# Attention in a fused layer: value products in every second step, from three tiles of turned exponentials

## The chip, the cores and the metric

The kernel runs on one core of one Trainium2 chip. The metric is the device time of one execution in microseconds (us). A core has five engines that run side by side, each with its own queue: TensorE (PE) multiplies matrices, VectorE (DVE) and ScalarE (ACT) work on elements, GpSimd (POOL) here issues the gathers by index, and SyncE (SP) issues most other transfers. PEld is PE's weight load, shown apart from the matmuls.

## The reference, cut to what matters

Two sequences of 4096 rows of 512 numbers go through a layer norm. Its result `xn` feeds an attention and a mixture of 16 experts, and the output is the sum of the input, the attention and the experts. All numbers are float32.

```
q, k, v = projections of xn, 64 wide, q and k rotated by position
scores = where(causal, q @ k.T / 8, -1e30)
attn = softmax(scores, axis=-1)
o = attn @ v
out_attention = o @ W_comp2lat.T @ W_to_kv + (o @ W_comp2lat.T) @ W_out_res.T + b_out_res
out_experts = shared expert + two of 16 experts per row, weighted
x = x + out_attention + out_experts
```

## The kernel before, in words

The work comes in four stages on one core. The first (to about 760 us) does norm, router, shared expert and projections. The second is a first attention pass over `p` = 0 to 6. The third is the experts (`gate_up`, `down`). The fourth is a second attention pass over `p` = 7 to 15, into which the last sums are woven. Both passes are one function, `attention` (line 773), called at lines 964 and 1137.

One `p` stands for two blocks of 128 queries in both sequences. Keys come in blocks of 128 too, and causality leaves `n = 2p + 2` of them. They are worked off two at a time, so a `p` has `M = p + 1` steps: 28 steps in the first pass, 108 in the second. A step does, in this order:

- `exps`: exponentials on ACT that this step needs and that are still waiting (line 756 works one piece of up to 1024 columns);
- `turn` (line 781): 16 small transposes on PE (line 790) of exponentials `E` into a PSUM tile `et` in two halves, and one copy per half to the SBUF tile `eT` (lines 796, 798, 799) on ACT, every fifth on DVE (every second for `p` = 15), as `copies` says. The halves take three PSUM banks in turn (`bank_of_three`);
- the sums that are due (`combine`, line 1104), in the second pass alone;
- a share of the scores of the next `p`: a chunk is 4 matmuls (line 740) and two reductions on DVE (lines 745, 748); the last two steps of a `p` have none, nor has `p` = 15;
- up to two exponentials of the next `p`;
- `products` (line 802) of the step before: 8 matmuls (line 810) that add `vv` times `eT` to the PSUM tile `oT`. After the last step of a `p`, DVE copies `oT` to `qT` (line 812). `oT` has one buffer.

The list `late` holds the one step whose products are still to come. PE, DVE and ACT keep the order in which the code names instructions (`manual_schedule`); SP's and POOL's order is made by a planner when the program is built, from its estimates and the free buffers.

`combine(p, i)` (due at the steps of line 1126: two for every seven) multiplies `qT` by `WO` (`po`, line 1112), and on DVE adds the rows of the experts and of `acc_d` (lines 1116, 1118); SP writes them out (line 1119). `load_parts` (line 1083) loads `acc_d` into tiles `fac` (line 1093, 12 buffers, four per `p`) and gathers two expert rows per token from `y_d` on POOL (line 1098): for `i` = 0 both are added onto `fac`, for `i` = 1 both go to a tile `fyy` of four. A group of four gathers therefore serves one `combine`: two for the first expert, two for the second, which add to what the first have brought. A half below is one `combine(p, i)`, part `p` with `i` = 0 or 1.

Of the kernel before, what the change touches and what calls it, by code (L numbers as in the profile page):

```python
# [8 lines left out]
F32 = mybir.dt.float32  # L9
# [10 lines left out]
P = 128  # L20
NB, T, D = 2, 4096, 512
# [31 lines left out]
def tile_mla_then_moe(  # L53
# [44 lines left out]
    def psO(name, second=False):  # L98
        return ps.tile([P, 512], F32, tag="T" if second else "O", name=name, bufs=1)
# [37 lines left out]
    at = ctx.enter_context(tc.tile_pool(name="at", bufs=2))  # L137
# [542 lines left out]
    def exps(n, upto=None):  # L680

        while waiting and (n > 0 or (upto is not None and min(waiting)[0] <= upto)):
            e = min(waiting)
            waiting.remove(e)
            e[2]()
            n -= 1
# [22 lines left out]
    def copies(p):  # L709

        turns[1] += 1
        return V.tensor_copy if turns[1] % (5 if p + 1 < NPR else 2) == 0 else S.copy
# [58 lines left out]
    H = P // 2  # L771

    def attention(E_tile, first, last, rows, extras, banks, copies, E_read=lambda t: None):

        late = []

        def turn(p, js, eT, n):

            pt = banks(f"et{p}_{js[0]}")
            for u, j in enumerate(js):
                for b in range(NB):
                    for i in range(1 if j == n - 1 else 0, 2):
                        o = u * 256 + (b * 2 + i) * H
                        for h in range(2):
                            e = slice(h * H, (h + 1) * H)
                            tr(pt[h][:, o:o + H],  # L790
                               rows[i][j // 8][e, b, (j % 8) * P:(j % 8 + 1) * P], ident[e, e])
            for h in range(2):
                copy = copies(p)
                dst = eT.rearrange("p u h b i q -> p (u h) (b i q)")
                if js[1] < n - 1:
                    copy(dst[:, h:h + 3:2, :], pt[h].rearrange("p (u c) -> p u c", u=2))  # L796
                else:
                    copy(dst[:, h, :], pt[h][:, 0:256])
                    copy(eT[:, 1, h, :, 1, :],
                         pt[h][:, 256:].rearrange("p (b i q) -> p b i q", b=NB, i=2)[:, :, 1, :])  # L800

        def products(p, oT, js, eT, n):
            for u, j in enumerate(js):
                for b in range(NB):
                    o, e = oT[b * DC:(b + 1) * DC, 0:256], eT[:, u, :, b]
                    if j == n - 1:
                        o, e = o.rearrange("d (h i q) -> d h i q", h=2, i=2)[:, :, 1], e[:, :, 1]
                    else:
                        e = e.rearrange("p h i q -> p h (i q)")
                    mm(out=o, lhsT=vv[j // 4][:, b, j % 4, :], rhs=e, start=(j == 0), stop=(j == n - 1))  # L810
            if js[-1] == n - 1:
                V.tensor_copy(
                    qT[p // 2][:, (p % 2) * 256:(p % 2 + 1) * 256].rearrange("d (i h q) -> d i h q", i=2, h=2),
                    oT[:, 0:256].rearrange("d (h i q) -> d i h q", h=2, i=2))

        for p in range(first, last):
            nxt, steps = score_steps(E_tile, p + 1, bank_pair) if p + 1 < last else (None, [])
            oT = psO(f"oT{p}")
            more = extras(p)
            n, M = 2 * p + 2, p + 1  # L820
            early = max(1, M - 2)
            pieces = sum(NB * -(-(n + 1 + i) // 8) for i in (0, 1)) if p + 1 < last else 0
            turn_of = 0.0
            for m in range(M):
                js = [2 * m, 2 * m + 1]

                exps(0, (p, min(js[1] + 2, n - 1) // 8))
                eT = at.tile([P, 2, 2, NB, 2, H], F32, tag="eT", name=f"eT{p}_{m}", bufs=2)
                turn(p, js, eT, n)
                for j in js:  # L830
                    if j % 8 == 7 or j == n - 1:
                        for i in range(2):
                            E_read(rows[i][j // 8])
                for f in more[len(more) * m // M:len(more) * (m + 1) // M]:
                    if f:
                        f()
                if m < early:
                    for f in steps[len(steps) * m // early:len(steps) * (m + 1) // early]:
                        f()
                turn_of = min(turn_of + pieces / M, 2.0)  # L840
                exps(int(turn_of), (p + 1, 0) if m == M - 1 else None)
                turn_of -= int(turn_of)
                if late:
                    late.pop()()
                late.append(lambda p=p, oT=oT, js=js, eT=eT, n=n: products(p, oT, js, eT, n))
            rows = nxt
        late.pop()()

    ring_k = ctx.enter_context(tc.tile_pool(name="rk", bufs=4))
    on_way = tc.tile_pool(name="wx", bufs=1)
    wx = on_way.__enter__()
# [106 lines left out]
    def fill(p):  # L961
        return filling.get(p, [])

    attention(E_first, 0, NPA, rows, fill, bank_of_three, copies)
    ring_a.__exit__(None, None, None)

# [101 lines left out]
    fin = ctx.enter_context(tc.tile_pool(name="fin", bufs=2))  # L1068
# [9 lines left out]
    def E_read(t):  # L1078
        live[:] = [e for e in live if e[1] is not t]
# [3 lines left out]
    def load_parts(p):  # L1083


        if p >= NPR:
            return
        tiles = {}
        for i in range(2):
            for b in range(NB):  # L1090
                j = b * (NT // NB) + 2 * p + i
                t = fin.tile([P, D], F32, tag="ac", name=f"fac{j}", bufs=12)
                nc.sync.dma_start(out=t, in_=acc_d[j * P:(j + 1) * P, :])
                y = t if i == 0 else fin.tile([P, D], F32, tag="yy", name=f"fyy{j}", bufs=4)
                tiles[i, b] = j, t, y
        for k in range(TOPK):
            for j, t, y in tiles.values():
                G.indirect_dma_start(  # L1098
                    out=y, out_offset=None, in_=y_d,
                    in_offset=bass.IndirectOffsetOnAxis(ap=pos[k][:, j:j + 1], axis=0),  # L1100
                    compute_op=ALU.bypass if y is not t and k == 0 else ALU.add)
        parts[p] = tiles

    def combine(p, i):

        if i == 0:
            load_parts(p + 2)
        qb = 2 * p + i
        po = psA(f"po{qb}")
        for b in range(NB):  # L1110
            e = slice(b * DC, (b + 1) * DC)
            mm(out=po[:, b, :], lhsT=qT[p // 2][e, (qb % 4) * P:(qb % 4 + 1) * P], rhs=WO[e, :],
               start=True, stop=True)
        for b in range(NB):
            j, a, y = parts[p][i, b]
            V.scalar_tensor_tensor(a, po[:, b, :], rl[:, b, qb:qb + 1], a, ALU.mult, ALU.add)
            if y is not a:
                V.tensor_tensor(a, a, y, ALU.add)  # L1118
            nc.sync.dma_start(out=out[j * P:(j + 1) * P, :], in_=a)
# [15 lines left out]
    for p in range(2):  # L1135
        load_parts(p)
    attention(E_rest, NPA, NPR, rows, sums_of, bank_of_three, copies, E_read)
    for i in range(2):
        combine(NPR - 1, i)
# [41 lines left out]
```

## Time and profile before

| | |
|---|---|
| median of 11 runs | 1978.75 us (1974.4 to 1984.36) |
| the profiled execution | 1978.63 us, span 1976.4 |
| busy in the span: PE, PEld, DVE, ACT, POOL | 96%, 71%, 55%, 32%, 29% |
| granted TensorE clock, mean | 0.992 |
| value matmuls, line 810 | 1088, of them 1024 on 256 columns: 393 ns each |
| transposes, line 790 | 2112, 231 ns each |
| copies of `eT` on ACT, line 796 | 186, 586 ns each |
| gathers of `fac`, of `fyy`, line 1098 | 64 each, 1570 and 1265 ns each |

The profile is one execution. A matmul's duration includes its way through the array, and matmuls overlap, so their cost is read from start to start. In a timeline a row is: start, duration of the merged instructions, engine, line, operation, output<-input, shapes, count, and in brackets how long the engine had stood idle and what is taken to have released it. In a list of waits a row is: engine and what it wanted, what it waited for, the total, the number of times and the longest.

### The profile page before, as it was taken

To read this page: it belongs to the slowest core of one execution; us is meant where nothing else is said; L and a number is where in the kernel's file an instruction comes from. 1 tells how busy PE (TensorE), PEld (TensorE's weight loads), DVE (VectorE), ACT (ScalarE), POOL (GpSimd) and SP (SyncE) were. 2 spreads that over 40 slices of the span, in tenths; PEclk is the share of its full clock that TensorE was granted. 3 is DMA by queue.
4 is the path that set the end of the run, shared out by engine and by line. 5 is a ranking of instruction groups with operands and counts; after the bars stand their busy time and mean duration, and the time that the engine had idled before them with its cause. 6 is when DMAs were issued, how large, how long until landed. Compare 5 with 4: busy or idle time off the path is not lost. (4 is left out here: it accounts for less than half of the span.)

```text
span 1976.4 us, 31902 instructions
## 1 busy us (share of the span) xinstructions
PE 1889.2 (96%) x12242; PEld 1404.7 (71%) x12242; DVE 1077.9 (55%) x2910; ACT 638.8 (32%) x1069; POOL 571.3 (29%) x499
## 2 busy tenths in 40 slices
PE   7999999999999987899999999999999999999996
PEld 6888888888888865467777777777777674444453
DVE  8878777778778776632222222222223325787774
ACT  2322232333222223531111111111111455666663
POOL 2333333323233341111111111111111105454554
PEclk9999999999999989999999999999999999999998
DMA  6222222322122213147888877878887767888887
GB/s 233 65 76 65 75 86 76 97 82 79 65 75 65 75 43 124 34 136 249 272 289 272 276 264 269 297 254 284 279 274 239 242 223 200 202 201 196 202 207 189
DMA packets 219435, 342.42 MB, mean 173 GB/s; under 512 B 19204, under 2 KB 109952, under 8 KB 219280
## 3 DMA queue, kind: packets, MB, share of 16 engines
q1 hardware_dynamic: 167600, 234.09, 36.7%
q0 software_dynamic: 31696, 69.99, 14.1%
q10 hardware_dynamic: 19984, 36.25, 4.8%
q8 instruction: 99, 1.62, 0.4%
q14 instruction: 56, 0.46, 0.1%
HBM read 250.22 MB, written 90.05 MB: 172 GB/s over the span
## 5 line engine op out<-in xcount | busy, mean ns | idle before, releaser
L1009 PE MATMUL pg<-xt,wgu 128*128 128x256 f32 (+1 forms) x2816 | 496.1, 335 | 0.0
L1009 PEld LDWEIGHTS pg<-xt,wgu 128*128 128x128 f32 x2816 | 434.8, 191 | 43.0 <-issue 0.5
L931 POOL DMA_INDIRECT xg<-xn_d,table x137 | 130.5, 952 | 684.3 <-DVE sw L991 553.4
L1015 DVE TENSOR_TENSOR eh<-esg,pg 128x512 f32<-128x512 f32 (+1 forms) x69 | 47.2, 684 | 394.8 <-ACT esg L1014 394.8
L1023 PE MATMUL py<-wdn,eh 128*128 128x512 f32 x548 | 247.1, 594 | 0.0
L986 DVE COPY xt<-pxt 128x512 f32<-128x512 f32 x138 | 88.3, 682 | 176.7 <-PE pxt L983 176.6
L1023 PEld LDWEIGHTS py<-wdn,eh 128*128 128x128 f32 x548 | 102.2, 190 | 106.6 <-issue 98.5
L756 ACT ACTIVATE E<-E,nb 128x1024 f32<-128x1024 f32 (+7 forms) x160 | 160.3, 1004 | 42.5 <-DVE nb L751 42.4
L1027 ACT ACTIVATE y<-py,sw 128x512 f32<-128x512 f32 x137 | 94.1, 687 | 231.1 <-PE py L1023 203.0
L748 DVE TENSOR_SCALAR_CACHE_REDUCE E<-s 128x512 f32<-128x512 f32 x224 | 143.6, 686 | 42.9 <-PE s L740 33.6
L1014 ACT ACTIVATE esg<-pg 128x512 f32<-128x512 f32 (+1 forms) x69 | 41.0, 594 | 380.6 <-PE pg L1009 332.9
L740 PE MATMUL s<-kT,qT 64*128 64x512 f32 (+3 forms) x576 | 142.7, 593 | 11.3 <-DVE E L748 7.3
L392 POOL DMA_INDIRECT order_d<-tok,at_u x128 | 129.1, 1009 | 64.6 <-issue 35.5
L810 PE MATMUL oT<-eT,vv 128*64 128x256 f32 x1088 | 144.0, 386 | 3.8 <-DVE eT L796 2.5
L790 PEld LDWEIGHTS et<-ident,E 64*128 64x128 f32 x2112 | 80.8, 139 | 78.7 <-issue 49.2
L796 ACT COPY eT<-et 128x512 f32<-128x512 f32 x186 | 102.0, 586 | 102.0 <-PE et L790 67.1
L810 PEld LDWEIGHTS oT<-eT,vv 128*64 128x64 f32 x1088 | 66.6, 136 | 93.7 <-issue 31.9
L790 PE MATMUL et<-ident,E 64*128 64x64 f32 x2112 | 102.6, 231 | 24.5 <-ACT eT L796 14.3
L1098 POOL DMA_INDIRECT fac<-y_d,pos_all x64 | 100.5, 1570 | 78.9 <-DMA fac<-y_d,pos_all 63.2
L353 POOL TENSOR_TENSOR x<-x,b_bc 128x2048 f32<-128x2048 f32 x16 | 76.1, 4756 | 147.1 <-DVE xn L350 134.3
L1098 POOL DMA_INDIRECT fyy<-y_d,pos_all x64 | 81.0, 1265 | 115.6 <-ACT eT L796 54.4
L460 ACT ACTIVATE gs<-gs 128x512 f32<-128x512 f32 x64 | 40.3, 630 | 182.4 <-DVE gs L479 69.3
(245 smaller groups left out, 2868.0 us busy)
## 6 DMA issues: line engine op xcount, KB each, us to landing
wgu<-in_L_ffn_gate_w_dram SPq DMA_DIRECT2D x88, 512.0 KB, 6.0
wgu<-in_L_ffn_up_w_dram SPq DMA_DIRECT2D x88, 512.0 KB, 8.8
wdn<-in_L_ffn_down_w_dram SPq DMA_DIRECT2D x88, 512.0 KB, 4.1
y_d<-y ACTq DMA_DIRECT2D x137, 256.0 KB, 6.0
xn_d<-xn SPq DMA_DIRECT2D x16, 1028.0 KB, 4.8
x<-in_L_attn_x_dram SPq DMA_DIRECT2D x16, 1024.0 KB, 6.7
acc_d<-x SPq DMA_DIRECT2D x16, 1024.0 KB, 5.3
fac<-acc_d SPq DMA_DIRECT2D x64, 256.0 KB, 5.1
```

Of the source, the lines that this page charges most:

```text
L392: G.indirect_dma_start(out=order_d[n % 4], out_offset=bass.IndirectOffsetOnAxis(ap=at_u[:, i, k:k + 1], axis=0), in_=tok[:, g * 4 + i, k:k ...
L740: mm(out=sc[b][:, 0:w], lhsT=q[e, :], rhs=kT[c][e, 0:w], start=True, stop=True)
L748: V.tensor_scalar(dst, sc[b][:, 0:w], SCALE, None, ALU.mult, ALU.max, accum_out=m)
L756: S.activation(E, E, AF.Exp, bias=nb[:, b:b + 1], accum_out=sm[:, b, c:c + 1])
L790: tr(pt[h][:, o:o + H], rows[i][j // 8][e, b, (j % 8) * P:(j % 8 + 1) * P], ident[e, e])
L796: copy(dst[:, h:h + 3:2, :], pt[h].rearrange("p (u c) -> p u c", u=2))
L810: mm(out=o, lhsT=vv[j // 4][:, b, j % 4, :], rhs=e, start=(j == 0), stop=(j == n - 1))
L931: G.indirect_dma_start(out=x_n, out_offset=None, in_=xn_d, in_offset=bass.IndirectOffsetOnAxis(ap=table[:, n:n + 1], axis=0))
L1009: mm(out=pg[:, g, f, at_s], lhsT=weights[u][0][:, c, g * FE + f * P:g * FE + (f + 1) * P], rhs=x_u[:, c, :], start=(c == 0), stop=(c == 3))
L1023: mm(out=py[:, v, :], lhsT=hT[:, c, v * P:(v + 1) * P], rhs=weights[u][1][:, c, :], start=(c == 0), stop=(c == 1))
L1027: S.activation(y, py[:, v, :], AF.Copy, scale=slot_w.pop(n))
L1098: G.indirect_dma_start(out=y, out_offset=None, in_=y_d, in_offset=bass.IndirectOffsetOnAxis(ap=pos[k][:, j:j + 1], axis=0), compute_op=ALU ...
```

## The change

`products` is no longer called in each step for the step before. The steps are counted over a whole call of `attention`; after each even one the products of all held steps but the newest are issued, two steps in one batch (one the first time). What is left at the end of the pass is issued there. So up to three `eT` tiles are alive, and they come from a pool of their own with three buffers, opened ahead of the `E` tiles, in place of two in `at`. A buffer is 4 KB per partition. `fac` goes from 12 buffers to 10, at 2 KB each.

```diff
+        count = [0]
...
-                eT = at.tile([P, 2, 2, NB, 2, H], F32, tag="eT", name=f"eT{p}_{m}", bufs=2)
+                eT = turned_E.tile([P, 2, 2, NB, 2, H], F32, tag="eT", name=f"eT{p}_{m}")
...
-                if late:
-                    late.pop()()
                 late.append(lambda p=p, oT=oT, js=js, eT=eT, n=n: products(p, oT, js, eT, n))
+                count[0] += 1
+                if count[0] % 2 == 0:
+                    for f in late[:-1]:
+                        f()
+                    del late[:-1]
...
-        late.pop()()
+        for f in late:
+            f()
...
+    turned_E = ctx.enter_context(tc.tile_pool(name="te", bufs=3))
...
-                t = fin.tile([P, D], F32, tag="ac", name=f"fac{j}", bufs=12)
+                t = fin.tile([P, D], F32, tag="ac", name=f"fac{j}", bufs=10)
```

In the built program SP and POOL follow. A load of `fac` stands behind the write-out of the half five before it, where it stood behind the half six before. On POOL the groups of `fac` and `fyy` alternate as before, but a `fac` group stands one `fyy` group later; the last four groups are `fac`, `fyy`, `fac`, `fyy` in whole, where before the third and second from last were interleaved.

## The prediction

> **What bounds the kernel now.** The profiled execution took 1978.63 us: a span of 1976.4 and 2.2 around it. The median of the runs shown is 1978.75 (1974.4 to 1984.36), so it stands at the median. On the page PE is busy 96%, which covers four stages. The change touches the first attention pass (764.9 to 859.8 us: p = 0 to 6, 28 steps) and the second (1641.9 on: p = 7 to 15, 108 steps). The expert stage between them starts when the first pass leaves PE, so what the first pass gains or loses moves all that follows.
>
> First view: PE's timeline in the second pass.
>
> ```profile
> 1802.46 0.71 PE L790 MATMUL et<-ident,E 64*128 64x64 f32 x16
> 1803.00 1.08 PE L740 MATMUL s<-kT,qT 64*128 64x512 f32 x4
> 1804.01 1.08 PE L810 MATMUL oT<-eT,vv 128*64 128x256 f32 x8
> 1805.03 0.71 PE L790 MATMUL et<-ident,E 64*128 64x64 f32 x16
> ```
>
> From start to start: 0.54 us of transposes, 1.01 of scores, 1.02 of values, without a pause. It looks as if PE set the pace. Second view: POOL's timeline at the end.
>
> ```profile
> 1933.18 1.00 POOL L1098 DMA_INDIRECT fyy<-y_d,pos_all  x1 [0.31 <-issue]
> 1934.48 0.96 POOL L1098 DMA_INDIRECT fyy<-y_d,pos_all  x1 [0.30 <-DVE fac L1116]
> 1939.11 1.57 POOL L1098 DMA_INDIRECT fyy<-y_d,pos_all  x1 [3.67 <-DMA fyy<-y_d,pos_all]
> 1940.98 1.56 POOL L1098 DMA_INDIRECT fyy<-y_d,pos_all  x1 [0.30 <-issue]
> 1942.84 1.54 POOL L1098 DMA_INDIRECT fac<-y_d,pos_all  x1 [0.30 <-issue]
> ```
>
> A group is four gathers: two first ones, a wait until they have landed, two that add. Between groups POOL pauses 0.30 us, whatever releaser is named. Third view: who POOL waited for from 1646 us on.
>
> ```profile
> POOL fac L1098 <- DMA fac<-y_d,pos_all: 63.2, 21, 5.4
> POOL fyy L1098 <- ACT eT L796: 54.4, 1, 54.4
> POOL fyy L1098 <- DMA fyy<-y_d,pos_all: 46.3, 14, 4.2
> ```
>
> The 54.4 lies before the pass (from 1592 to 1646.58, until the experts' rows are written). All else is its own landings: never a free buffer, never a sum on DVE. So the gathers are one unbroken chain from 1646.58 to the last landing at 1972.25, 325.7 us at their own pace. Fourth view: DVE's timeline, where the sums take the gathered rows.
>
> ```profile
> 1963.86 0.69 DVE L1118 TENSOR_TENSOR fac<-fac,fyy 128x512 f32<-128x512 f32 x1 [0.78 <-DMA fyy<-y_d,pos_all]
> 1964.47 0.42 DVE L812 COPY qT<-oT 128x256 f32<-128x256 f32 x1
> ...
> 1972.31 0.69 DVE L1118 TENSOR_TENSOR fac<-fac,fyy 128x512 f32<-128x512 f32 x1 [1.42 <-DMA fyy<-y_d,pos_all]
> ```
>
> DVE waits for gathers; PE then waits 3.61 us for that copy. The second pass ends with POOL; PE is about 5 us early (3.6 here, 1.4 before L1118).
>
> **The change part by part.**
>
> *Switches saved.* Values work on 128 rows, transposes and scores on 64 (128*64 and 64*128 in the rows), and PE pays for changing between them. Eight value matmuls are four pairs 0.216 apart. Alone they take 1.015 us. At the end of the first pass sixteen stand together from 858.18 to 859.85: 1.67, and as the narrower last eight take 0.80 alone (1797.32 to 1798.12), the others took 0.865, so 0.15 less. A chunk of scores takes 1.01 before values and 0.91 before more of its kind: 0.10 less. Together 0.25 per group that disappears. The first pass has 28 groups before and 15 after, the second 108 and 55: 13 x 0.25 = 3.2 us and 53 x 0.25 = 13.2. The bounds of the 0.25 are 0.15, if transposes after scores restart as slowly as after values, and 0.30, if their first interval shortens too. What is moved are value matmuls and at an end of p one copy on DVE; no DMA goes with them. The third eT tile suffices: the copy that refills a tile comes a step after the matmuls that read it.
>
> *Transposes that come too early.* In a step without values the next transposes come 1.1 us sooner. Their banks are three in turn, so they need the bank that this step's first copy empties. In the step at 1802.46 that copy ends at 1803.84, 1.19 before the next transposes: just enough. A step with two chunks has 2.0. But a step with neither scores nor sums (849.31 to 850.97) has 0.27, so it loses about 0.85: mostly the last two steps of each p, and most of p = 15. Behind the waiting transposes stand this step's scores or sums and the sixteen value matmuls, so DVE gets its scores later by as much. Where exponentials stand ahead of the copy on ACT there is none (the wait of 3.3 for E at L756 is such a place). Going through the steps after which values are left out and adding what is short of 1.1: 6.4 us in the first pass, 14 in the second.
>
> *qT's copy.* oT has one buffer. Where one p ends and the next begins inside one batch, PE stands still until DVE has copied oT (L812), and in the changed order that copy stands behind the new step's DVE work. This is so six times: after steps 6 and 10 of the first pass, and 8, 38, 50 and 92 of the second. Price: at 1798.67 the copy now runs before the step's work; behind one copy, four sums (1800.69 to 1803.56) and two reductions it would end near 1805.3, and PE wants it at 1802.2: 3 us. With two reductions alone (1.37 + 0.42, less 0.4 of remaining scores) it is 1.4. Bounds 1.4 to 3.5 each, so 3 to 7 in the first pass and 6 to 14 in the second; I take 11 for the second, as two of its four places have sums.
>
> *First pass.* Its terms alone give -3.2 + 6.4 + 3 to 7, that is +6 to +10, but waits overlap. Walking steps 22 to 28 (p = 6) by the rows: transposes at 848.3 instead of 847.37, 849.7 (849.31), 852.2 (850.97), then exponentials on ACT hold both orders, 857.4 (856.01), 858.85 (857.67), end 862.0 (859.85): +2.1. The same walk through steps 4 to 21 gives +1.9. I take **+4.0**, between -3.2 (only gain) and +10.
>
> *Second pass on PE.* -13.2 + 14 + 11 = +11.8.
>
> *Pool of their own.* New addresses; the waits that DVE's first scores carry stand in both orders alike, and their longest now is 2.0 us. I take 0 between -2 and +2.
>
> *Ten buffers for fac.* Each load on SP now follows the write-out five halves back, not six. Loads come 16 us ahead of their gather now (issued at 1899.7, landed 5.1 later, gathered at 1920.86), so one half (10 us) less is still covered; without that cover POOL would wait up to 10 us a part. But POOL's own order changes too: fac of a part now stands behind the previous part's fyy. The work is equal except at the end. Now the last fac and the last but one fyy interleave: 1942.84 to 1959.16, 16.3 us. In the changed order they stand one after the other: the eleven fac groups from 1710 to 1942.84 last 11.65 on average, the eleven fyy groups 9.51, together 21.2. That is **+4.85**, between 0 and +6.
>
> [...]
>
> **The sum.** 1978.63 + 4.0 (POOL starts later) + 4.85 (its chain is longer) = **1987.5 us**. PE's +11.8 is covered by its 5 us and the 4.85, and by sums that no longer wait for fyy: only just.
>
> **The rivals.**
>
> *PE gains and the end follows.* Then POOL's pauses would have to shrink with PE. All terms but the switches at zero: 1978.6 - 16.5 = 1962. Against it: the third view. For it: nothing but how small the other terms are each.
>
> *Nothing moves.* The first pass comes out even, since an earlier score feeds DVE and ACT earlier, and landings overlap as now: 1978.6, within 4 us.
>
> *Slower, PE the bound.* The six copies cost 3.5 each and no shortfall is absorbed: first pass +10.2, second -13.2 + 14 + 14 = +14.8 less PE's 5: 1978.6 + 10.2 + 9.8 = 1998.6. It decides as soon as the second pass costs PE over 9.85 us, and my +11.8 before relief is near that.
>
> **Chances.** My forecast 0.46, the slow rival 0.24, no change 0.17, faster 0.13. A measurement can tell about 0.2% (4 us) from none; 0.02 of the forecast falls within that. Slower 0.68, same 0.19, faster 0.13. The range leaves out the fast rival and the far end of the slow one: 1974 to 2001.
>
> **What would show it.** Value groups of sixteen, 1.88 us from start to start: the saving is real. Waits of transposes for ACT's copies (now 14.3 us) should about double, and a new wait of values for qT (now 1.2) reach 8 to 18. The first pass should last 99 us instead of 94.9. POOL should pause for landings alone and its last landing be about 1981. I am wrong if POOL is found waiting for loads of fac or ends well before DVE's last sum, or if the first pass gets shorter.

## The result and the profile after

The changed kernel takes 2003.94 us (median; 2000.86 to 2007.56), the kernel before 1980.38 on the same chip: a ratio of 1.0118 [1.0107, 1.0129]. The direction was as forecast, the size was not: 23.6 us in place of 8.8, beyond the range. Its profiled execution took 2005.36 us with a span of 2003.5, 27.1 more than before. Lines behind the edit are numbered 1 to 8 higher now (790 is 791, 796 is 797, 810 is 811, 812 is 813, 1116 is 1124, 1118 is 1126).

First, PE's timeline in the second pass of the changed kernel, where the prediction showed the even rhythm of before:

```profile
1843.36 0.71 PE L791 MATMUL et<-ident,E 64*128 64x64 f32 x16
1843.91 1.08 PE L740 MATMUL s<-kT,qT 64*128 64x512 f32 x4
1844.82 0.69 PE L791 MATMUL et<-ident,E 64*128 64x64 f32 x16
1845.32 2.22 PE L740 MATMUL s<-kT,qT 64*128 64x512 f32 x8
1847.46 1.95 PE L811 MATMUL oT<-eT,vv 128*64 128x256 f32 x16
1849.34 0.71 PE L791 MATMUL et<-ident,E 64*128 64x64 f32 x16
```

The sixteen values take 1.88 us from start to start, as predicted. But the pair of steps takes 5.98 where the same pair took 6.00 before. The 0.25 that was saved is in the line at 1845.32: two chunks of scores take 2.14 to the next start, 1.87 elsewhere. The second of them needs the bank that the chunk of 1843.91 filled; DVE's reductions of that chunk end at 1846.34, and the second chunk starts at 1846.40. A pair with one chunk in each step (steps 3 and 4 of p = 13) does show the saving: 4.87 after, 5.14 before.

Second, who POOL waits for in the second pass of the changed kernel (the answer that was the third view of the prediction):

```profile
POOL fac L1106 <- DMA fac<-y_d,pos_all: 60.6, 26, 5.6
...
POOL fyy L1106 <- DMA fyy<-y_d,pos_all: 43.0, 14, 4.4
POOL fyy L1106 <- DVE fac L1126: 14.0, 12, 3.9
...
POOL fyy L1106 <- DMA fac<-acc_d: 6.5, 7, 1.8
```

Two rows that stood at 0.3 us each before have grown: POOL waits for sums on DVE (14.0) and for loads of `fac` (6.5). Its chain no longer sets the pace. How far off the end it is, the timelines of POOL, then of DVE and PE at the end show:

```profile
1984.85 1.56 POOL L1106 DMA_INDIRECT fyy<-y_d,pos_all  x1 [0.42 <-issue]
```

```profile
1994.33 0.42 DVE L813 COPY qT<-oT 128x256 f32<-128x256 f32 x1
1994.80 1.99 PE L1120 MATMUL po<-WO,qT 64*128 64x512 f32 x8 [0.77 <-DVE qT L813]
...
1999.47 0.69 DVE L1126 TENSOR_TENSOR fac<-fac,fyy 128x512 f32<-128x512 f32 x1
```

The last gather is issued 15 us before the last sum, and that sum waits for PE's values, their copy and `po`. PE now sets the end. What PE waits for in the second pass, before and after:

```profile
PE et L790 <- ACT eT L796: 9.9, 9, 2.8
PE po L1112 <- DVE qT L812: 3.6, 1, 3.6
PE s L740 <- DVE E L748: 3.0, 4, 0.8
...
PE s L740 <- DVE fac L1116: 2.5, 3, 1.4
```

```profile
PE et L791 <- ACT eT L797: 15.9, 17, 2.2
PE oT L811 <- DVE qT L813: 10.2, 4, 3.4
PE s L740 <- DVE fac L1124: 6.5, 8, 1.2
PE s L740 <- DVE E L748: 3.2, 5, 0.8
```

The 10.2 in four places is the copy of `qT`, at the four ends of a p that the prediction named. In the first pass the same wait is small, before (first line) and after (second):

```profile
PE oT L810 <- DVE qT L812: 1.2, 1, 1.2
```

```profile
PE oT L811 <- DVE qT L813: 1.7, 2, 1.0
```

One of the four, after step 50 (PE and DVE of the changed kernel):

```profile
1824.33 0.87 PE L811 MATMUL oT<-eT,vv 128*64 128x256 f32 x8
1824.36 0.69 DVE L1126 TENSOR_TENSOR fac<-fac,fyy 128x512 f32<-128x512 f32 x1
...
1826.97 0.69 DVE L748 TENSOR_SCALAR_CACHE_REDUCE E<-s 128x512 f32<-128x512 f32 x1
...
1827.58 0.42 DVE L813 COPY qT<-oT 128x256 f32<-128x256 f32 x1
1828.15 1.98 PE L811 MATMUL oT<-eT,vv 128*64 128x256 f32 x8 [2.95 <-DVE qT L813]
```

PE stands still for 2.95 us. And the eight values that follow take 1.98 us where eight took 0.87 a moment before. The granted clock (the share of full speed that PE is given) says why (PE's stretches of the changed kernel: length, PE busy, clock, DMA share, GB/s):

```profile
1820.00:1830.00 10.00, 6.33 (x52) 0.86 0.98 244
1830.00:1840.00 10.00, 10.00 (x100) 0.80 0.69 162
```

The clock was at half from 1827.25 to 1834.07. The same view of all engines (busy PE, PEld, DVE, ACT, POOL, then clock, DMA share, GB/s) shows it strongest in the first pass, before (first line) and after (second):

```profile
765.00:860.00 95.00, 78.35 (x784) 43.77 (x786) 54.98 (x202) 58.10 (x134) 13.22 (x14) 0.95 0.24 76
```

```profile
765.00:872.00 107.00, 85.15 (x770) 48.72 (x771) 55.52 (x201) 58.44 (x136) 13.21 (x14) 0.82 0.22 69
```

PE is busy longer in the second row though its matmuls are fewer. Taken to the last end of the pass, with the same 782 matmuls, PE is busy 78.4 us before and 86.4 after, and idle 16.7 and 21.4: of the 12.8 us that the pass grew, 8.0 are busy time and 4.8 idle.

A list of waits leaves out what is merged into a row, such as the 0.27 above. So I took every distance between two starts on PE and called a wait what it has above a fixed distance for that succession (0.50 between pairs of scores, most of which start 0.42 to 0.49 apart at full clock; 0.29 between pairs of values, most 0.21 to 0.26 apart; 0.06 between transposes, and so on). At half clock some of the longer distance is counted as a wait. In us, from the profiled executions:

| | first pass, before | after | second pass, before | after |
|---|---|---|---|---|
| waits of transposes | 13.8 | 18.9 | 13.5 | 24.9 |
| waits of scores and po | 7.3 | 10.9 | 13.4 | 19.5 |
| waits of values | 1.3 | 5.3 | 3.5 | 11.1 |
| all else (matmuls, switches) | 72.5 | 72.6 | 295.4 | 285.7 |
| sum: PE from first to last start | 94.9 | 107.7 | 325.8 | 341.2 |
| of it at half clock | 10.2 | 37.5 | 6.8 | 13.7 |

The switches are saved in the second pass (9.7 us), and 25 us of waits stand against them. In the first pass the saving and the waits can't be read from this table, since half clock lengthens both. So I counted the same distances a second time: at half clock, what lies within twice that distance is half work and half loss to the clock, and only the rest is a wait. The difference between after and before is then, in us:

| | first pass | second pass |
|---|---|---|
| matmuls and switches, as at full clock | -3.4 | -10.5 |
| loss to half clock | +11.7 | +3.1 |
| waits of transposes | +3.3 | +9.2 |
| waits of scores and po | +0.6 | +6.2 |
| waits of values | +0.5 | +7.2 |

This is an accounting of one pair of executions, and in this pair the clock differs more than usual: 63.6 us at half clock in the whole execution after and 32.5 before, where the means of all runs are 55.7 and 40.8.

### The profile page after: what moved, and what is told of

Its sections match the earlier page's. It is cut to its first block, busy times and chain, and to the rows that moved or that the text cites. A ratio compares the mean times of both kernels' runs of the same rounds, so it can differ in the third digit from the quotient of the medians.

```text
span 2003.5 us, 31900 instructions
## 1 busy us (share of the span) xinstructions
PE 1892.6 (94%) x12242; PEld 1421.2 (71%) x12242; DVE 1078.4 (54%) x2910; ACT 637.7 (32%) x1069; POOL 569.8 (28%) x499
## 5 line engine op out<-in xcount | busy, mean ns | idle before, releaser
L740 PE MATMUL s<-kT,qT 64*128 64x512 f32 (+3 forms) x576 | 153.3, 627 | 16.8 <-DVE E L748 8.1
L791 PEld LDWEIGHTS et<-ident,E 64*128 64x128 f32 x2112 | 88.4, 143 | 92.6 <-issue 38.3
L811 PE MATMUL oT<-eT,vv 128*64 128x256 f32 x1088 | 135.5, 391 | 11.9 <-DVE qT L813 11.9
L791 PE MATMUL et<-ident,E 64*128 64x64 f32 x2112 | 104.4, 233 | 36.7 <-ACT eT L797 21.1
L811 PEld LDWEIGHTS oT<-eT,vv 128*64 128x64 f32 x1088 | 74.2, 141 | 81.7 <-issue 47.9
L306 PE MATMUL gu<-xnT,Wg 128*128 128x256 f32 x384 | 96.2, 388 | 2.0 <-ACT gs L471 1.3
```

What stands on the lines that cost most here:

```text
L306: mm(out=o[:, r, :], lhsT=lhs[:, c, r * P:(r + 1) * P], rhs=rhs[:, c, :], start=c == 0, stop=c == 1)
L740: mm(out=sc[b][:, 0:w], lhsT=q[e, :], rhs=kT[c][e, 0:w], start=True, stop=True)
L791: tr(pt[h][:, o:o + H], rows[i][j // 8][e, b, (j % 8) * P:(j % 8 + 1) * P], ident[e, e])
```

## The experiments

Theory W: PE sets the end, and the values in every step were the cover under which DVE and ACT emptied PE's banks. Rival M: the memory side (addresses, ten `fac` buffers) costs the time. Rival G: the waits matter most through the clock that they bring down. All ratios are to the kernel before on the same chip.

### Each part of the change by itself

**every_step**

```diff
-                if count[0] % 2 == 0:
+                if True:
```

> Values are issued in every step again, as before the change; the eT pool of three and the ten fac buffers stay. Theory W (PE sets the end; the values were the cover under which DVE and ACT emptied PE's banks, and without them PE waits): the order of PE is that of before, so the first pass takes 94.9 us again and the time is 1980, or up to 1985 if the ten buffers lengthen POOL's chain by the 4.85 us of the prediction. Rival M (memory side: new addresses and fewer fac buffers cost the time): about 2000, with the first pass near 95 and POOL waiting for loads of fac.

Measured: 1979.27 us, ratio 0.9987 [0.9969, 1.0005]; first pass 96.1 us. M falls: pool, addresses and ten buffers cost nothing. So does the prediction's +4.85 for POOL's tail: the last sums of this run wait for gathers, so POOL's chain sets its end, and the interval leaves room for 1 us more than before. (From the first gather of `fac` in the second pass to the last gather's issue POOL takes 311.6 us, 314.9 before; one profile each, which is too little to call it shorter.)

**first_only** and **second_only**

```diff
-                if count[0] % 2 == 0:
+                if first > 0 or count[0] % 2 == 0:
```

and in the other kernel `first == 0`.

> Batches of two steps in the first pass alone; values in every step in the second. Theory W: the first pass is longer by the 13.3 us that POOL's first gather of the second pass came later, and nothing is given back, since POOL's chain starts that much later: 1993, up to 1998 with the 4.85 of the ten buffers. Rival M: as the kernel with values in every step, whatever that shows. Rival G (the loss is the half clock that pauses of PE bring, 37.5 us of it in the first pass of after and 10.2 in that of before): the first pass's loss follows the time at half clock in this run's own profile, about 0.4 us per us of it.

> Batches in the second pass alone; values in every step in the first. Theory W: the first pass is 94.9 us, the second loses on PE what it lost in after, 27.0 of span less 13.3, so about 13.7: 1994. The two parts add up: this and the kernel with batches in the first pass alone give, above the one with values in every step, together the 24 us of after. Rival M: no difference from values in every step. My prediction's picture (POOL's chain is the bound, PE covered) would give 1985.

Measured: 1992.5 us, 1.0047 [1.0026, 1.0068], and 1996.21 us, 1.0066 [1.0044, 1.0089]. Above every_step these are 0.0060 and 0.0079, together 0.0139; the whole change is 0.0131 above it. Both passes lose, and the losses add up. In second_only the prediction's cover would have left 1985. In the profile of first_only, POOL's chain sets the end, as the prediction had it: the last gather is issued at 1985.67, 9.4 us after PE's last matmul, and POOL waits for its own landings alone. It takes 321.0 us there, 9.4 more than in every_step with the same order, so its length varies by this much from one profile to the next.

### The copy of qT

**two_oT** gives `oT` two halves of one bank in turn.

```diff
+        both = psO(f"oT{first}")
...
-            oT = psO(f"oT{p}")
+            oT = both[:, p % 2 * 256:p % 2 * 256 + 256]
```

> The changed kernel with two oT tiles, halves of the one bank, in turn: values of the next p need not wait until DVE has copied the last. Theory W: the waits of values for qT go (they rose from 1.3 to 5.3 us in the first pass and from 3.5 to 11.1 in the second), at most 13 us in all: 1991 if nothing comes in their place, 1998 if half of it turns into waits for the scores' banks. Rival G: the three stretches at half clock in the second pass each follow such a wait, so they go too, and up to 4 us more. If the qT waits were not the loss: 2003.

Measured: 2005.65 us, 1.0117 [1.0093, 1.0142]. The list of PE's waits in its second pass still has the row that was to go:

```profile
PE oT L812 <- DVE qT L814: 10.2, 4, 3.4
```

So the built program still waits for the copy; the edit took nothing away, and the run says nothing about the cause. Another edit does:

**cut_same**

```diff
+                if m == 0 and len(late) > 1:
+                    late.pop(0)()
+                    if len(late) > 1:
+                        late.pop(0)()
                 if count[0] % 2 == 0:
```

> The changed kernel, but where one p ends and the next begins inside a batch, the last eight values of the old p are issued one step earlier, by themselves; all other batches stay. (The kernel with two oT halves kept its waits for qT: 11.5 us in the second pass, so it did not take them away; this one does.) Theory W: values wait for qT 4 us less in the first pass and 9 less in the second, six more switches cost 1.5: 1993. If the wait moves on to the next resource instead (the scores' banks behind DVE's queue): 2000 or more. [...]

Measured: 1989.21 us, 1.0034 [1.0019, 1.0049]. PE's waits in its second pass (L1128 is the sum at L1124 of the changed kernel):

```profile
PE et L791 <- ACT eT L797: 15.2, 16, 2.2
PE s L740 <- DVE fac L1128: 6.6, 8, 1.2
```

The wait for `qT` is gone, nothing took its place, and the others stand as in the changed kernel. The second pass is 12.3 us shorter on PE and the first 7.9, for six places where a batch is cut. In the medians it is 0.84% of 1980 us, 17 us (13 to 20 by the two intervals), where the two lists have 11.9 us of waits for `qT`. Half clock fell too: in the profiles from 37.5 to 17.1 us in the first pass and from 13.7 to 10.2 in the second, in the mean of all runs from 55.7 to 49.7 us in all.

### The transposes

**scored_only**

```diff
-                if count[0] % 2 == 0:
+                if m % 2 == 0 or m >= early:
```

The steps `m` of a p from `early` on are its last two.

> Values are held back only in every second step of a p and only in steps that have scores (in p = 15, in all but the last two), so no batch reaches over the end of a p: 49 groups fewer than before instead of 66. Theory W: waits for qT go, waits of transposes for ACT's copies fall to near the 14 us of before in both passes, waits of scores stay at 17 in the second pass; the first pass has only 6 batches of two steps and lasts 95 to 98 us. PE's second pass about 327 us: 1980 to 1986. If the loss came from every left-out group alike: 49/66 of 24 us above before, 1998.

Measured: 1980.67 us, 0.9993 [0.9978, 1.0008]. PE's waits in its second pass:

```profile
PE et L791 <- ACT eT L797: 11.3, 9, 3.1
PE s L740 <- DVE fac L1124: 7.6, 11, 1.3
```

Waits of transposes are back to 16.3 us (23.2 in cut_same, 16.1 in every_step). Against cut_same 8 us more of the loss are gone: they came from values held back in the last two steps of each p, which scored_only issues in every step again. The switches are still saved (286.2 against 295.1), but waits of scores and po (20.7 against 9.4) take all of it: PE's second pass is 324.8 us, in every_step 321.6.

### The scores' banks

**values_ahead** and **scored_ahead** issue the sixteen values ahead of the step's last chunk, the first with the changed kernel's batches, the second with those of scored_only. This is the heart of the first one's change; `part` holds the chunks of scores of the step.

```diff
...
+                for f in part[:-1] if batch else part:
+                    f()
+                if batch:
+                    for f in late[:-1]:
+                        f()
+                    del late[:-1]
+                    for f in part[-1:]:
                         f()
...
```

> The changed kernel with the same batches, but in a step with a batch the sixteen values are issued ahead of the step's last chunk of scores and not behind it, so that DVE has their 1.9 us to empty the bank which that chunk needs. Theory W: waits of scores, 17.5 us in the second pass and 10.9 in the first, fall back to the 8 and 7 of before; qT's copy has one chunk's two reductions less ahead of it: 2004 less 10 to 15, so 1989 to 1994. If the scores' banks were not the cause: no change, 2004.

> As the kernel that holds values back only in steps with scores, and the sixteen values ahead of the step's last chunk of scores. Theory W: no wait is left that before has not, and the switches are saved: PE's second pass 316 to 320 us instead of 325.8, first pass 95. Then POOL's chain of gathers sets the end again, and little of it shows: 1976 to 1981. If PE alone set the end: 1970.

Measured: 2015.02 us, 1.0146 [1.0111, 1.0181], and 1988.4 us, 1.0023 [1.0010, 1.0036]: the first slower than the changed kernel, the second slower than scored_only. The half of the expectation on scores held: their waits in the second pass fell from 17.5 to 8.3 and from 16.1 to 8.1 us. But those of transposes rose from 24.9 to 36.7 and from 16.3 to 27.7. Who ACT waits for suggests why: in the changed kernel (first line) and in values_ahead (second):

```profile
ACT E L756 <- DVE nb L751: 21.7, 10, 3.0
```

```profile
ACT E L756 <- DVE nb L751: 30.0, 11, 4.8
```

Where the late chunk ends its row of blocks, the row's maximum and so its exponentials are late by the values' 1.9 us, and they stand ahead of the next copies of `eT` on ACT. **ahead_inner** tests this: cut_same, with the values ahead only where the chunk does not end its row.

```diff
+                steps[-1].final = c == nch - 1
...
+                ahead = part and not part[-1].final
```

> The kernel whose batches are cut where a p ends, and the sixteen values go ahead of the step's last chunk of scores only where that chunk does not end its row of blocks. In the kernel that put them ahead everywhere the waits of scores fell from 17.5 to 8.3 us, but those of transposes rose from 24.9 to 36.7. Theory: where the chunk ends a row, exponentials hang on it, they are 1.9 us late and stand ahead of the copies on ACT. If so, here the waits of transposes stay near the 23 of the cut kernel, those of scores fall from 16.4 to about 11, PE's second pass from 328.9 to 324, and the time from 1989 to 1984. If the late chunk itself delays the transposes: 1995 or more.

Measured: 1988.48 us, 1.0032 [1.0015, 1.0049]. On PE's second pass the theory holds in its numbers: waits of transposes 25.1, of scores 10.8, the pass 324.9 us. The total, for which 1984 was expected, does not follow. In the profiled run the first pass is longer, 102.8 us against 99.8, with 27.3 us at half clock against 17.1. And the last two sums wait for gathers (1.40 and 1.48 us), which they don't in cut_same: with a shorter second pass on PE, POOL's chain sets the end again.

| second pass on PE, us | transposes | scores, po | values | all else | sum | first pass |
|---|---|---|---|---|---|---|
| every_step | 16.1 | 9.4 | 1.1 | 295.1 | 321.6 | 96.1 |
| scored_only | 16.3 | 20.7 | 1.7 | 286.2 | 324.8 | 97.4 |
| ahead_inner | 25.1 | 12.1 | 1.3 | 286.4 | 324.9 | 102.8 |
| cut_same | 23.2 | 18.4 | 1.7 | 285.6 | 328.9 | 99.8 |
| after | 24.9 | 19.5 | 11.1 | 285.7 | 341.2 | 107.7 |

### The clock

**filler_every** (values in every step) and **filler_after** (the changed kernel) add matmuls that compute nothing, to keep PE busy in three waits for exponentials at the start of the first pass.

```diff
+            def filler(k):
+                for _ in range(k):
+                    mm(out=pt[1][0:H, 256:512], lhsT=ident[0:H, 0:H], rhs=kT[0][0:H, 0:256], start=True, stop=True)
+            filler(12 if p == 0 else 0)
...
+                        if (u, b, i, js[0]) == (0, 0, 0, 0):
+                            filler({1: 7, 3: 4}.get(p, 0))
```

> Values in every step, and 23 matmuls that compute nothing (4 kinds of places in the first pass: 12 ahead of p = 0's transposes, 7 after the first transposes of p = 1, 4 after those of p = 3), put where PE waits for exponentials; they write parts of the et bank that the real transposes overwrite. PE's work grows by about 5 us, all of it inside waits. [...] If the fillers push the transposes back: up to 5 us more.

> The changed kernel with the same 23 matmuls that compute nothing. Rival G: the long stretch at half clock from 766 to 783 us goes, half clock in the first pass falls from 37.5 to about 20 us, and the time by 0.4 us per us, about 7 us: 1997. Theory W alone: the waits are as before, 2004.

Measured: 1978.8 us, 0.9986 [0.9971, 1.0000], and 2004.76 us, 1.0111 [1.0080, 1.0143]: no change clear of the noise. But the fillers were too long. PE's timeline of filler_after at the start of the first pass:

```profile
764.45 5.39 PE L788 MATMUL et<-kT,ident 64*64 64x256 f32 x24
769.77 0.59 PE L797 MATMUL et<-ident,E 64*128 64x64 f32 x12
```

Twelve are 24 instructions and 5.39 us in a wait of 3.3: they pushed the pass back by about 2 us. **filler_half_after** and **filler_half_every** have half as many (6, 3 and 1 in place of 12, 7 and 4).

> The changed kernel with 10 fillers instead of 23 (6 ahead of p = 0, 3 in p = 1, 1 in p = 3); each is two matmuls of 0.2 us, so they take 2.6, 1.3 and 0.4 us in waits of 3.3, 1.7 and 0.5. Rival G: half clock in the first pass falls by 10 us or more, and the time by 0.4 us for each: 1998 or less. Theory W alone (half clock there lies beside the waits for exponentials): 2004.

> Values in every step, with the same 10 fillers. Rival G: half clock in the first pass falls from 13.7 us to 7 or less and the time from 1979 to 1976, below both kernels. Theory W alone: 1979.

Measured: 2057.1 us, 1.0181 [1.0121, 1.0240], and 2029.21 us, 1.0018 [0.9990, 1.0047]. Beside them the kernel before itself took 2026 us, most of the difference ahead of the first pass, so these numbers can't be set beside the others. The same two kernels again:

> As the run before of the changed kernel with 10 fillers. Rival G: half clock in the first pass falls from 37.5 us by 10 or more, and the time by 0.4 us for each: a ratio to before of 1.009 or less. Theory W alone: 1.012 as without fillers.

> As the run before of values in every step with 10 fillers. Rival G: ratio to before 0.997 or less. Theory W alone: 0.9987 as without fillers.

Measured: 2001.01 us, 1.0127 [1.0097, 1.0158], and 1974.03 us, 0.9982 [0.9968, 0.9995]. In the profiled run of filler_half_after_2 the fillers fit, and the same two rows read:

```profile
757.95 2.80 PE L788 MATMUL et<-kT,ident 64*64 64x256 f32 x12
761.28 0.28 PE L797 MATMUL et<-ident,E 64*128 64x64 f32 x2 [0.53 <-ACT E L756]
```

From the first score to the last value of the first pass it takes 107.8 us, of them 20.5 at half clock; the changed kernel takes 111.7, with 37.5. So 17.0 us less at half clock went with 3.9 us less time there. In the whole time this does not show: 1.0127 is no less than 1.0118, and in that profile the second pass on PE is 3.4 us longer than after's (344.6 against 341.2). G's ratio of 1.009 is excluded, if narrowly. But the mean of the four runs is 51.0 us at half clock, against 36.5 of the kernel before beside them: 14.5 us more, as without fillers. So the fillers did not take the clock's part away here, and the run can't price it. In the four runs of filler_after they did: 42.1 us at half clock, 41.7 of the kernel before beside them. Its ratio is 1.0111 all the same, of which some 0.001 is the 2 us by which the fillers pushed the pass back. So most of the loss is there without more half clock. The second kernel is the only one here whose interval lies below 1, but it can't be told from every_step.

There is a second witness. All executions list their mean clock. Taken as made up of 1 and 0.5 alone, which is all that the profiles of before and after have, 2 x (1 - clock) x span is the time at half clock. Within one kernel, from run to run, the time rises by 0.43 us (+-0.06; 187 runs of 15 kernels, without those at 2026 us and beside them) per us of it. The changed kernel has 55.7 us on average, the kernel before 40.8. An estimate from these: 14.9 x 0.43 = 6 us of the 24 go with the clock. By the same slope it is more in the first pass: first_only has 54.1 us at half clock on average and every_step 40.8, so 5.7 of the 13.2 us between them; second_only has 46.3, so 2.4 of its 16.9.

## Why the prediction was wrong

Two steps failed most: the term of the first pass, +4.0 where 12.8 was measured, and the cover under which the second pass's loss was to vanish. A third, waits for the scores' banks, was missing.

**Switches saved: right in kind, a little less in size.** -13.2 was forecast for the second pass; -9.7 (or -10.5 by the second count) measured, 0.18 to 0.20 a group in place of 0.25. In the first pass -3.2 was forecast and -3.4 is found by the second count.

**qT's copy: right in place; right in size in the second pass alone.** The six places were named. In the second pass 11 us were forecast and 10.2 found in the list of waits. In the first pass 3 to 7 were forecast, but two places cost 1.7, where before had 1.2 already. Taking the six places away gave 17 us back, more than their 11.9; an estimate for the clock's part is 6.0 us of half clock x 0.43 = 2.6.

**Transposes that come too early: right in kind, too high in size.** +6.4 and +14 were forecast; +5.1 and +11.4 measured, of which the second count leaves +3.3 and +9.2. In the lists, waits for ACT's copies of whole steps rose from 14.3 to 21.1 us and did not double. scored_only shows the place: the last two steps of a p.

**The scores' banks: missing.** No term of the sum had them. Its part on what is moved went through the banks of `et` and through `oT`, and not through the third resource that PE fills, the two pairs of banks of scores and po. Waits of scores alone rose by 9.4 us in the second pass (partly offset at po, where the 3.6 us for POOL's late sums at the end of before went away), about what the switches save. In the first pass they rose by 3.6, most of it half clock. values_ahead shows the cause in the second pass: with 1.9 us more for DVE, 9.2 of these 17.5 us went, only to come back at the transposes.

**The first pass, +4.0: the step that failed most.** Its terms stood at +6 to +10, and the walk by hand then let them overlap to +2.1 and +1.9. Measured: 12.8 by the profiles. The waits were not too low: +4.0 with -3.2 for the switches leaves 7.2 for them, and PE's idle time rose by 4.8. What the walk had at nothing, without a reason, is the clock: it took every duration at full clock, where 37.5 us were at half (10.2 before). PE was busy 8.0 us longer on the same matmuls, and the second count puts 11.7 of the 12.8 down to half clock. This pair of profiles shows the clock at its strongest; by the slope from run to run it is about 6 of 13 us.

**"PE's +11.8 is covered by its 5 us and the 4.85".** The second pass cost PE 15.4 us, beyond the 9.85 from which the slow rival was to decide. And the 4.85 was not there, as every_step shows. With no chain of POOL's to hide under, PE's loss came through whole, as the slow rival said. Its figure, 1998.6, was 5 short, and near in part by luck: it had 7 us for copies of `qT` in the first pass, which cost 0.5 more than before, and neither the scores' banks nor the clock. Both signs that the prediction named for being wrong appeared: POOL waits for loads of `fac`, and it ends well before the last sum.

What stays open: how much of the first pass's loss the clock causes, since no run took half clock away and left all else alone; what makes up the 17 us of the six places beyond their waits; and whether two `oT` buffers would do the same, since two_oT did not take the wait away. Why the second pass of filler_half_after_2 took longer was not pursued either.

## What to carry to other kernels

Work that is moved out of a step takes its cover along: list every buffer that the engine fills in that step and ask, one by one, who empties it and when, not only the buffers of the moved work. When a batch reaches over a boundary where a single accumulator is read out, the read-out stands behind the next block's work on its engine; cutting the batch there is cheap (six switches here) and was worth 17 us. And price new pauses twice: as idle time, and by the granted clock of the stretch behind them. A walk through the steps at full clock priced the idle time of the first pass rather too high (7.2 us for 4.8) and missed its longer busy time (8.0).

## What the runs showed of the hardware

In the profiles of before and after the granted TensorE clock is 1 or 0.5 throughout. It falls to 0.5 in 7 places before and in 11 after. Each time but the last, which runs on past the end, it is back at 1 after 3.41 us, or 2, 3 or 5 times that. Of the 3.41 us ahead of such a place the records of matmuls cover 0 to 0.59 in 17 of the 18, and 0.79 in one. Of all other stretches of 3.41 us at full clock, counted from where the clock changes, 14 are covered by less than 0.6, each by 0.50 to 0.59. In the last 3.41 us at half clock before full clock came back, the cover is 0.83 to 1.00 in all 16 places. At half clock the starts in the changed kernel lie twice as far apart: 0.42 us for a pair of values (0.21 at full clock), 0.85 for a pair of scores (0.42 to 0.43).

In the second pass of the changed kernel half clock began at 1690.71, 1714.61 and 1827.25 us and lasted 3.41, 3.41 and 6.83. In the 3.41 us ahead PE was busy for 1.23, 1.50 and 1.37 us. The longest waits that ended there were 3.35 us for `qT` ahead of the first, 1.68 for a copy of `eT` ahead of the second and 2.95 for `qT` ahead of the third. So the wait of 2.95 us was not all that was lost there: for 5.92 us behind it matmuls started at half the pace.
